# Inverse Haar column transforms of the first 16 channels moved to VectorE, half of the coefficient sums moved to GpSimd

## Chip, cores and metric

The kernel runs on one core of a Trainium2 chip. The metric is device time in microseconds (us) of one execution; lower is better. Four compute engines matter: TensorE (PE; its weight loads are listed as PEld), VectorE (DVE), ScalarE (ACT) and GpSimd (POOL). SyncE's queue (SP) and ACT's queue issue the DMAs.

## What is computed

Input x has shape (4, 64, 256, 256), float32: 4 batches, 64 channels, images of 256 by 256. Four layers follow each other.

- Layers 0, 1 and 3 are the same kind: a long two-dimensional convolution of each channel with a separable filter that a small sine network makes, plus the input times a bias per channel. As the filter is separable, it is two one-dimensional causal convolutions, one along each axis.
- Layer 2 goes through a two-dimensional Haar transform:

```python
f1 = haar2d(x)
for i in range(2):
    f4 = einsum('bchw,oc->bohw', f1 * v[i], conv_w[i])
    acc = acc + sign(f4) * relu(abs(f4) - tau[i])
y = haar2d(acc, inverse=True) + x
```

So each coefficient position mixes the 64 channels by two 64 by 64 matrices, each of the two results is soft-thresholded, and the two are added.

## The kernel before

A convolution of layers 0, 1 or 3 along one axis is one `contract` (two pairs of matmuls against a Toeplitz tile read from DRAM), so a layer takes two: `a` then `y`. ACT copies the first product out of PSUM (L275), VectorE adds the residual to the second (L292).

For each batch b there are three stages.

**convolutions(b)**: per channel, layers 0 and 1 (`a0`, `y0`, `a1`, `y1`), then the Haar transform along rows on VectorE (lengths 128 and 64, L350 and L351) and on GpSimd (lengths 32 to 2, the same two lines, ten instructions for each four channels), then along columns on TensorE (`down`, tile `pz`, with the numbers split by ACT and VectorE into two fp32r parts, `sp`). Coefficients go to DRAM (`coef`), sums and differences for later (`keep`).

**mixing(b)**: 64 groups g of two coefficient rows each (q = 0, 1). Per group: TensorE multiplies by the two matrices (`px`), VectorE and ACT scale (L468, L473), ACT takes the absolute value into `mag` (L477) and the sign (L480), VectorE subtracts the threshold (`shrink`, L484) and multiplies by the sign (`signed`, L488). `add` (L494) sums the two terms into `z`, one instruction of 128 by 256 for each q, both on VectorE. The tile `mag` has two buffers, so the Abs of group g + 2 needs the adds of group g. `z` holds a whole batch in SBUF: four chunks of 16 channels, 128 coefficient rows, 256 columns' worth in each partition.

**inverse(b)**: the inverse Haar transform along columns, in two different ways:

- Channels 16 to 63 (chunks 1 to 3 of `z`): VectorE does it in place in `z`. `level(n, chunk)` is one of seven steps, n = 1, 2, 4 ... 64; it works on n pairs of rows with two instructions in `halve` (L299, L300). An instruction covers up to 16 pairs here, 128 by 1024.
- Channels 0 to 15 (chunk 0): no levels. After the row transform, `halves` splits the PSUM result into two fp32r parts (ACT cast L548, VectorE subtraction L549, tile `w`), and `cols` multiplies both by a matrix (TensorE L555, tile `pu`, two matmuls of 512 columns per channel). This takes one tick more before the join.

Per channel c: `fetch` copies the channel's column from `z` (ACT, L534), `rows` does the row transform on TensorE (L541, L542, tile `pw`), `join` combines it with `r`, loaded from `keep` (VectorE L563, L566, L567), and layer 3 follows (`a3`, `y3`), with the result stored. In batches 0 to 2 every third channel from 2 on stops after the join; its result is stored to `late`, and layer 3 for these 63 images runs alongside the mixing of batch 3 (tile `v`).

**Order.** Every step is put into a list with a time in ticks (`at`; the offsets are the table `PLACE`), sorted and emitted. The order in the list is a priority: a scheduler then lays out each engine's instructions, and an instruction whose inputs are there may be placed ahead of others that wait. While batch b is mixed, the convolutions of batch b + 1 run beside it; a group of the mixing takes one tick, a channel of the inverse too. `along` is the tick at which the mixing of the batch starts, `start` the tick at which its inverse starts.

Of the kernel before, what the change touches and what calls it, by code (L numbers as in the profile page):

```python
# [12 lines left out]
ALU = mybir.AluOpType  # L13
# [3 lines left out]
B, C, S, EMB, ORD = 4, 64, 256, 33, 64  # L17
# [8 lines left out]
PLACE = {  # L26
    "load": 0.714,
    "a0": 1.643,
    "a0 copy": 1.643,
    "y0": 2.571,  # L30
    "y0 sum": 2.571,
    "a1": 3.5,
    "a1 copy": 3.5,
    "y1": 4.429,
# [63 lines left out]
def conv_seq_kernel(ctx, tc, x, fz, fw, bias, decay, haar, haar_row, factors, vt, taut, wmix, out):  # L98
# [14 lines left out]
    nc = tc.nc  # L113
# [22 lines left out]
    z = zpool.tile([P, 4, P, 4, 16], F32, name="z")  # L136
# [21 lines left out]
    order = mybir.DependencyInfo(mybir.DependencyClass.NoSync, mybir.DependencyReason.DATA)  # L158
# [135 lines left out]

        return [product, residual]

    def halve(even, odd):

        nc.vector.tensor_sub(odd, even, odd)  # L299
        nc.vector.scalar_tensor_tensor(even, even, 2.0, odd, ALU.mult, ALU.subtract)  # L300

    def level(n, chunk, begin=0, count=None):

        count = n if count is None else count
        v = z.rearrange("p n s x c -> p n s (x c)")[:, chunk].rearrange("p (j e s) x -> p j e s x", e=2, s=P // 2 // n)
        halve(v[:, begin : begin + count, 0, 0, :], v[:, begin : begin + count, 1, 0, :])

    def butterfly():

        v = z.rearrange("p n s (h k) c -> p n s h k c", k=2)  # L310
        for h in range(2):
            halve(v[:, :, 0, h, 0, :], v[:, :, 0, h, 1, :])
# [6 lines left out]
    def at(time, run, unit):  # L319
        events.append((time, len(events), run, unit))  # L320
# [104 lines left out]
    def mixing(b, start, n_act):  # L425

        st = {}

        def load(g):
            f = mx.tile([P, 2, S], F32, name=f"f_{b}_{g}", tag="f", bufs=3)  # L430
            nc.sync.dma_start(f, coef[b].rearrange("k c p w -> (k c) p w")[:, 2 * g : 2 * g + 2])
            st[g] = {"f": f}
            if g % GT == 0:
                t = mx.tile([P, 2, GT, 16], F32, name=f"vt_{b}_{g}", tag="vt")
                nc.sync.dma_start(t, scales[g // GT])
                st["vt", g // GT] = t

        def scale(g, i):
            return st["vt", g // GT][:, i, g % GT, :]

        def over(g, i, n):
            return scale(g, i)[:, :n].unsqueeze(2).to_broadcast([P, n, C])

        def mix(g):
            f = st[g]["f"]
            ps = psx.tile([P, 2, 2, S], F32, name=f"px_{b}_{g}", tag="mix")
            for q in range(2):
                for h in range(2):
                    nc.tensor.matmul(  # L449
                        ps[:, q, h, :],  # L450
                        f[:, q, h * P : (h + 1) * P],
                        wb.rearrange("p r n -> p (r n)"),
                        start=True,
                        stop=True,
                    )
            if g == 0:

                one, two = ps[:, 0, :, :P], ps[:, 0, :, P:]
                d = mx.tile([P, 2, P], F32, name=f"d_{b}", tag="mag")
                nc.vector.tensor_copy(d, two)  # L460
                nc.vector.tensor_sub(two, one, d)
                nc.vector.tensor_add(one, one, d)
            st[g]["f4"] = mx.tile([P, 16, C], F32, name=f"f4_{b}_{g}", tag="f4")
            st[g]["px"] = ps.rearrange("p q h (r i o) -> p (q h r i) o", r=2, i=2)

        def scaled(g):
            px, n = st[g]["px"], 16 - n_act
            nc.vector.tensor_tensor(st[g]["f4"][:, :n], px[:, :n], over(g, 0, n), ALU.mult)  # L468

        def scaled_too(g, half):  # L470
            px, f4 = st[g]["px"], st[g]["f4"]
            for j in range(16 - n_act + half * (n_act // 2), 16 - (1 - half) * (n_act - n_act // 2)):
                nc.scalar.mul(f4[:, j], px[:, j], scale(g, 0)[:, j : j + 1])  # L473

        def size(g):
            mag = st[g]["mag"] = mx.tile([P, 16, C], F32, name=f"mag_{b}_{g}", tag="mag")
            nc.scalar.activation(mag, st[g]["f4"], AF.Abs)  # L477

        def sign(g):
            nc.scalar.activation(st[g]["f4"], st[g]["f4"], AF.Sign)  # L480

        def shrink(g):
            mag = st[g]["mag"]
            nc.vector.tensor_sub(mag, mag, over(g, 1, 16))  # L484

        def signed(g):
            mag = st[g]["mag"]
            nc.vector.scalar_tensor_tensor(mag, mag, 0.0, st[g]["f4"], ALU.max, ALU.mult)  # L488

        def add(g):  # L490
            parts = st.pop(g)["mag"].rearrange("p (q x i) (n c) -> p q i x n c", q=2, i=2, n=4)
            for q in range(2):
                to = slot(2 * g + q)
                nc.vector.tensor_add(  # L494
                    z[:, :, to].rearrange("p n x c -> p x n c"), parts[:, q, 0], parts[:, q, 1]
                )


        for g in range(S // 4):
            for name, stage in zip(  # L500
                ("mix load", "mix", "scaled", "scaled too", "scaled rest", "size", "sign", "shrink", "signed", "add"),
                (
                    load,
                    mix,
                    scaled,
                    lambda g: scaled_too(g, 0),
                    lambda g: scaled_too(g, 1),
                    size,
                    sign,
                    shrink,  # L510
                    signed,
                    add,
                ),
            ):
                at(start + g + PLACE[name if b + 1 < B else "l " + name], stage, g)

    def inverse(b, start, put_off):

        st = {}

        def early(c):
            tag, bufs = ("f", 3) if c < 20 or c % 5 < 3 else ("f4", 2)
            r = mx.tile([P, 2, 2, P], F32, name=f"r_{b}_{c}", tag=tag, bufs=bufs)
            nc.sync.dma_start(r, keep[b][c])
            st[c]["r"] = r
# [34 lines left out]
        def join(c):  # L560
            ps = st[c]["pw"]
            t = io.tile([P, 2, 2, P], F32, name=f"t_{b}_{c}", tag="res", bufs=BUFS["res"])
            nc.vector.scalar_tensor_tensor(t, st[c]["r"], 0.5, ps, ALU.mult, ALU.add)  # L563
            u = io.tile([P, 2, S], F32, name=f"u_{b}_{c}", tag="y", bufs=BUFS["y"])
            v = u.rearrange("p m (w e) -> p m w e", e=2)
            nc.vector.tensor_add(v[:, :, :, 0], t[:, 0], t[:, 1])  # L566
            nc.vector.tensor_sub(v[:, :, :, 1], t[:, 0], t[:, 1])  # L567
            st[c]["u"] = u
# [4 lines left out]
        along = start - groups - 3  # L573

        def when(tick, n, chunk, *span):
            at(tick + PLACE["level"], lambda _: level(n, chunk, *span), 0)

        at(along + 11 + PLACE["level"], lambda _: butterfly(), 0)
        for chunk in range(1, 4):
            turn = start + 16 * (chunk - 1)  # L580
            for n in (1, 2, 4, 8):
                when(along + 12 + 3 * chunk if b + 1 < B else turn, n, chunk)
            when(turn + 1, 16, chunk)
            for i in range(2):
                when(turn + 2 + 2 * i, 32, chunk, 16 * i, 16)
            for i in range(4):
                when(turn + 6 + 2 * i, 64, chunk, 16 * i, 16)

        for c in range(C):
            for name, stage in zip(("sooner", "early", "fetch", "rows"), (sooner, early, fetch, rows)):  # L590
                at(start + c + PLACE[name], stage, c)
            turn = start + c
            if c < 16:
                at(start + c + PLACE["halves"], halves, c)
                at(start + c + PLACE["cols"], cols, c)
                turn += 1
            at(turn + PLACE["join"], join, c)
            if c in put_off:
                at(turn + PLACE["aside"], aside, c)
            else:  # L600
                shift = (0.0, 0.0)
                if put_off:
                    shift = ((-0.27, -0.342), (0.23, 0.158))[c % 3]
                for name, stage in zip(("a3", "a3 copy", "y3", "y3 sum", "out"), last(b, st)):
                    at(turn + PLACE[name] + shift[name[0] != "a"], stage, c)
# [59 lines left out]
    ahead = C  # L665
    start = ready + 3
    for b in range(B):
# [10 lines left out]
        start = max(end + C, ready + 3)  # L678
        ahead = start - 3
# [114 lines left out]
```

## Time and profile before

| | us |
|---|---|
| median of 3 runs | 2875.76 |
| lowest, highest | 2874.41, 2878.55 |
| the profiled execution, time | 2874.07 |
| the profiled execution, span of the trace | 2872.3 |
| PE busy | 2827.1 |
| DVE busy | 2494.9 |
| ACT busy | 2080.3 |
| POOL busy | 334.4 |

The page lists for each engine how long it was busy; the span is what the trace covers, the time includes what lies around it (1.8 us). Groups of instructions are listed by line, engine and tile, with the number of instructions, the busy time, the mean duration in ns, and the idle time before them with what ended it. A line of a timeline has the start, the time until the end of the last of the merged instructions, the engine, the line, what is written from what is read, and how many instructions it merges. A window's row has the busy time of each engine in that window.

### The profile page before, as it was taken

To read this page: it belongs to the slowest core of one execution; us is meant where nothing else is said; L and a number is where in the kernel's file an instruction comes from. 1 tells how busy PE (TensorE), PEld (TensorE's weight loads), DVE (VectorE), ACT (ScalarE), POOL (GpSimd) and SP (SyncE) were. 2 spreads that over 40 slices of the span, in tenths; PEclk is the share of its full clock that TensorE was granted. 3 is DMA by queue.
4 is the path that set the end of the run, shared out by engine and by line. 5 is a ranking of instruction groups with operands and counts; after the bars stand their busy time and mean duration, and the time that the engine had idled before them with its cause. 6 is when DMAs were issued, how large, how long until landed. Compare 5 with 4: busy or idle time off the path is not lost. (4 is left out here: it accounts for less than half of the span.)

```text
span 2872.3 us, 52434 instructions
## 1 busy us (share of the span) xinstructions
PE 2827.1 (98%) x16592; PEld 2555.6 (89%) x16592; DVE 2494.9 (87%) x4255; ACT 2080.3 (72%) x4950; POOL 334.4 (12%) x644
## 2 busy tenths in 40 slices
PE   9999999999999999999999999999999999999999
PEld 7899998898888898998898998998898998888998
DVE  4655558999999779999999779999999779999985
ACT  2333338999995558998985658999995659998554
POOL 0111111121121001221221001121121000000000
PEclk9999999999999999999999999999999999999999
DMA  6878787776667986777777986777777988787786
GB/s 182 249 231 230 232 232 227 207 208 204 205 209 213 289 254 198 214 213 214 209 207 236 299 255 196 213 214 216 208 208 235 297 266 235 229 238 212 224 241 201
DMA packets 599367, 649.77 MB, mean 226 GB/s; under 512 B 48465, under 2 KB 517044, under 8 KB 598964
## 3 DMA queue, kind: packets, MB, share of 16 engines
q1 hardware_dynamic: 536996, 578.61, 68.9%
q10 hardware_dynamic: 62096, 67.82, 6.7%
q8 instruction: 134, 2.20, 0.3%
q14 instruction: 141, 1.16, 0.1%
HBM read 426.77 MB, written 219.48 MB: 225 GB/s over the span
## 5 line engine op out<-in xcount | busy, mean ns | idle before, releaser
L261 PE MATMUL py<-t,a 128*128 128x256 f32 x3072 | 922.5, 382 | 9.5 <-ACT a L275 8.7
L275 ACT COPY a<-pa 128x512 f32<-128x512 f32 x768 | 478.8, 623 | 498.6 <-PE pa L262 455.2
L473 ACT ACTIVATE f<-px,vt 128x64 f32<-128x64 f32 x2816 | 610.5, 367 | 101.6 <-DVE f L468 101.1
L262 PEld LDWEIGHTS py<-t,a 128*128 128x128 f32 x3072 | 583.4, 190 | 79.3
L262 PE MATMUL py<-t,a 128*128 128x128 f32 x3072 | 590.0, 274 | 0.0
L261 PEld LDWEIGHTS py<-t,a 128*128 128x128 f32 x3072 | 497.3, 191 | 51.2 <-ACT a L275 19.0
L449 PE MATMUL px<-wb,f 128*128 128x256 f32 x2048 | 487.6, 380 | 7.6 <-ACT f L473 7.6
L449 PEld LDWEIGHTS px<-wb,f 128*128 128x128 f32 x2048 | 369.0, 190 | 50.0 <-ACT f L473 10.5
L351 POOL TENSOR_TENSOR sd<-less 128x128 f32<-128x128 f32 (+4 forms) x320 | 190.8, 596 | 1858.7 <-DVE less L350 1519.9
L534 ACT COPY zc<-z 128x512 f32<-128x512 f32 x256 | 282.1, 1105 | 108.1 <-PE pw L542 99.0
L484 DVE TENSOR_TENSOR mag<-mag,vt 128x1024 f32<-128x1024 f32 x256 | 316.6, 1237 | 12.3 <-ACT mag L477 11.5
L488 DVE SCALAR_TENSOR_TENSOR mag<-mag,f 128x1024 f32<-128x1024 f32 x256 | 316.6, 1238 | 0.0
L261 PE MATMUL pa<-t,y 128*128 128x256 f32 x1024 | 309.1, 384 | 6.8 <-DVE y L292 5.2
L261 PE MATMUL pa<-t,x 128*128 128x256 f32 x1024 | 305.9, 381 | 0.5 <-DMA t<-pad 0.5
L477 ACT ACTIVATE mag<-f 128x1024 f32<-128x1024 f32 x256 | 295.7, 1155 | 2.8 <-DVE z L494 0.4
L374 DVE TENSOR_TENSOR sp<-sd,sp 128x512 fp32r<-128x512 f32 x256 | 179.8, 702 | 129.3 <-ACT sp L369 128.2
L480 ACT ACTIVATE f<-f 128x1024 f32<-128x1024 f32 x256 | 285.8, 1116 | 3.5
L261 PE MATMUL pa<-t,u 128*128 128x256 f32 x772 | 233.2, 384 | 6.5 <-ACT w L548 2.8
L292 DVE SCALAR_TENSOR_TENSOR y<-x,bsb,py 128x512 f32<-128x512 f32 x256 | 190.9, 746 | 41.9 <-PE py L262 41.0
L262 PEld LDWEIGHTS pa<-t,x 128*128 128x128 f32 x1024 | 194.6, 190 | 26.3
L262 PEld LDWEIGHTS pa<-t,y 128*128 128x128 f32 x1024 | 194.5, 190 | 26.3
L292 DVE SCALAR_TENSOR_TENSOR y<-y,bsb,py 128x512 f32<-128x512 f32 x256 | 190.7, 745 | 26.0 <-PE py L262 25.6
(73 smaller groups left out, 4412.3 us busy)
## 6 DMA issues: line engine op xcount, KB each, us to landing
t<-pad SPq DMA_DIRECT2D x768, 256.0 KB, 4.1
x<-in_x SPq DMA_DIRECT2D x256, 256.0 KB, 3.7
coef<-co SPq DMA_DIRECT2D x256, 256.0 KB, 3.2
f<-coef SPq DMA_DIRECT2D x256, 256.0 KB, 3.2
r<-keep SPq DMA_DIRECT2D x256, 256.0 KB, 4.1
out_y<-y ACTq DMA_DIRECT2D x193, 256.0 KB, 4.3
keep<-sums SPq DMA_DIRECT2D x256, 128.0 KB, 2.8
keep<-sd SPq DMA_DIRECT2D x256, 128.0 KB, 2.8
```

The source lines that it names most:

```text
L261: nc.tensor.matmul(ps[:, m, :], src[:, 0, m * P : (m + 1) * P], t[:, ::-1], start=True, stop=False)
L262: nc.tensor.matmul(ps[:, m, P:], src[:, 1, m * P : (m + 1) * P], t[:, : P - 1 : -1], start=False, stop=True)
L275: nc.scalar.copy(a, s["p" + new])
L292: nc.vector.scalar_tensor_tensor(y, s[res], bsb[:, layer, c : c + 1], s["p" + new], ALU.mult, ALU.add)
L351: engine.tensor_tensor(t[:, :, :, half:length], v[..., 0], v[..., 1], ALU.subtract)
L449: nc.tensor.matmul(ps[:, q, h, :], f[:, q, h * P : (h + 1) * P], wb.rearrange("p r n -> p (r n)"), start=True, stop=True,)
L473: nc.scalar.mul(f4[:, j], px[:, j], scale(g, 0)[:, j : j + 1])
L477: nc.scalar.activation(mag, st[g]["f4"], AF.Abs)
L480: nc.scalar.activation(st[g]["f4"], st[g]["f4"], AF.Sign)
L484: nc.vector.tensor_sub(mag, mag, over(g, 1, 16))
L488: nc.vector.scalar_tensor_tensor(mag, mag, 0.0, st[g]["f4"], ALU.max, ALU.mult)
L534: nc.scalar.copy(a.rearrange("p h k i -> p (h k) i"), z[:, c // 16, :, :, c % 16].rearrange("p i x -> p x i"))
```

## The change

In batches 0 to 2, chunk 0 gets levels like the other three, and `halves` and `cols` are no longer emitted for channels 0 to 15; their join is one tick earlier. The last batch keeps `halves` and `cols`. The levels of batches 0 to 2 get new places: all levels of chunk 0 but the last eight pairs, those of chunk 1 up to half of n = 64, and those of chunks 2 and 3 up to n = 16 are placed within the mixing; the rest within the inverse, in pieces of 8 pairs (128 by 512). From `start` on, a piece gets a scheduling order (no semaphore) behind the last join emitted before it. In the mixing of batches 0 to 2, the add of q = 1 goes to GpSimd for all groups but the last two; in batch 3 both adds do. The buffers for `r` use tag `f4` from channel 4 on instead of channel 20 in batches 0 to 2.

```diff
-    def halve(even, odd):
+    behind = [None]
+    order = mybir.DependencyInfo(mybir.DependencyClass.NoSync, mybir.DependencyReason.DATA)
 
-        nc.vector.tensor_sub(odd, even, odd)
+    def halve(even, odd, stay=False):
+
+        first = nc.vector.tensor_sub(odd, even, odd)
+        if stay and behind[0] is not None:
+            tc.add_manual_dep(first.ins, behind[0].ins.name, order, reason="not ahead of the joins")
         nc.vector.scalar_tensor_tensor(even, even, 2.0, odd, ALU.mult, ALU.subtract)
...
                 to = slot(2 * g + q)
-                nc.vector.tensor_add(
-                    z[:, :, to].rearrange("p n x c -> p x n c"), parts[:, q, 0], parts[:, q, 1]
-                )
+                engine = nc.gpsimd if g + 2 < S // 4 and (q or b + 1 == B) else nc.vector
+                engine.tensor_add(z[:, :, to].rearrange("p n x c -> p x n c"), parts[:, q, 0], parts[:, q, 1])
...
-            tag, bufs = ("f", 3) if c < 20 or c % 5 < 3 else ("f4", 2)
+            tag, bufs = ("f", 3) if c < (4 if b + 1 < B else 20) or c % 5 < 3 else ("f4", 2)
...
-            nc.vector.scalar_tensor_tensor(t, st[c]["r"], 0.5, ps, ALU.mult, ALU.add)
+            behind[0] = nc.vector.scalar_tensor_tensor(t, st[c]["r"], 0.5, ps, ALU.mult, ALU.add)
...
+        def piece(tick, n, chunk, begin, count):
+            at(tick + PLACE["level"], lambda _: level(n, chunk, begin, count, stay=tick >= start), 0)
+
         at(along + 11 + PLACE["level"], lambda _: butterfly(), 0)
-        for chunk in range(1, 4):
-            turn = start + 16 * (chunk - 1)
-            for n in (1, 2, 4, 8):
-                when(along + 12 + 3 * chunk if b + 1 < B else turn, n, chunk)
-            when(turn + 1, 16, chunk)
-            for i in range(2):
-                when(turn + 2 + 2 * i, 32, chunk, 16 * i, 16)
+        if b + 1 < B:
+            for chunk in range(4):
+                for n in (1, 2, 4, 8):
+                    when(along + 12 + 3 * chunk, n, chunk)
+                when(along + 20 + 3 * chunk, 16, chunk)
+            for chunk in range(2):
+                for i in range(2):
+                    when(along + 37 + i + 3 * chunk, 32, chunk, 16 * i, 16)
+                for i in range(3 - chunk):
+                    when(along + 43 + 8 * i + 3 * chunk, 64, chunk, 16 * i, 16)
+            when(along + 63, 64, 0, 48, 8)
+            when(start - 0.2, 64, 0, 56, 8)
             for i in range(4):
-                when(turn + 6 + 2 * i, 64, chunk, 16 * i, 16)
+                piece(start + 4 + 2 * i, 64, 1, 32 + 8 * i, 8)
+            for chunk in range(2, 4):
+                turn = start + 20 * chunk - 32
+                for i in range(4):
+                    piece(turn + i, 32, chunk, 8 * i, 8)
+                for i in range(8):
+                    piece(turn + 4 + 2 * i, 64, chunk, 8 * i, 8)
+        else:
+            for chunk in range(1, 4):
...
-            if c < 16:
+            if c < 16 and b + 1 == B:
                 at(start + c + PLACE["halves"], halves, c)
                 at(start + c + PLACE["cols"], cols, c)
                 turn += 1
```

The branch behind the last `else` is the old placing of chunks 1 to 3, now for the last batch alone.

More of the change, by code (lines that the diff above doesn't have):

```diff
@@ L295, in second, with level @@
         return [product, residual]
-    def halve(even, odd):
-        nc.vector.tensor_sub(odd, even, odd)
+    behind = [None]
[4 more added lines that the diff above has]
+            tc.add_manual_dep(first.ins, behind[0].ins.name, order, reason="not ahead of the joins")
         nc.vector.scalar_tensor_tensor(even, even, 2.0, odd, ALU.mult, ALU.subtract)
-    def level(n, chunk, begin=0, count=None):
+    def level(n, chunk, begin=0, count=None, stay=False):
         count = n if count is None else count
         v = z.rearrange("p n s x c -> p n s (x c)")[:, chunk].rearrange("p (j e s) x -> p j e s x", e=2, s=P // 2 // n)
-        halve(v[:, begin : begin + count, 0, 0, :], v[:, begin : begin + count, 1, 0, :])
+        halve(v[:, begin : begin + count, 0, 0, :], v[:, begin : begin + count, 1, 0, :], stay)
     def butterfly():
@@ L576, in when @@
             at(tick + PLACE["level"], lambda _: level(n, chunk, *span), 0)
+        def piece(tick, n, chunk, begin, count):
+            at(tick + PLACE["level"], lambda _: level(n, chunk, begin, count, stay=tick >= start), 0)
         at(along + 11 + PLACE["level"], lambda _: butterfly(), 0)
-        for chunk in range(1, 4):
-            turn = start + 16 * (chunk - 1)
-            for n in (1, 2, 4, 8):
-                when(along + 12 + 3 * chunk if b + 1 < B else turn, n, chunk)
-            when(turn + 1, 16, chunk)
-            for i in range(2):
-                when(turn + 2 + 2 * i, 32, chunk, 16 * i, 16)
-            for i in range(4):
-                when(turn + 6 + 2 * i, 64, chunk, 16 * i, 16)
+        if b + 1 < B:
[10 more added lines that the diff above has]
+            when(start - 0.2, 64, 0, 56, 8)
+            for i in range(4):
+                piece(start + 4 + 2 * i, 64, 1, 32 + 8 * i, 8)
[7 more added lines that the diff above has]
+            for chunk in range(1, 4):
+                turn = start + 16 * (chunk - 1)
+                for n in (1, 2, 4, 8):
+                    when(turn, n, chunk)
+                when(turn + 1, 16, chunk)
+                for i in range(2):
+                    when(turn + 2 + 2 * i, 32, chunk, 16 * i, 16)
+                for i in range(4):
+                    when(turn + 6 + 2 * i, 64, chunk, 16 * i, 16)
         for c in range(C):
```

## The prediction, made before the change was run

> **What bounds the kernel now.** I read the page's busy shares first, then the stages, then single instructions.
>
> ```profile
> PE 2827.1 (98%) x16592; PEld 2555.6 (89%) x16592; DVE 2494.9 (87%) x4255; ACT 2080.3 (72%) x4950; POOL 334.4 (12%) x644
> PEclk9999999999999999999999999999999999999999
> ```
>
> TensorE is busy 98% at the full granted clock, so only less TensorE work or less TensorE idling can shorten the run. To see how near the other engines are, I cut the trace at the first Abs (L477) of a mixing, its last add into z (L494), the fetch of channel 16, and the next mixing. Columns: window, length, then busy time of PE, PEld, DVE, ACT, POOL, clock, DMA share, GB/s. The rows are mixing 0, inverse 0 up to channel 16, its rest, mixing 1, inverse 1 up to channel 16, mixing 3.
>
> ```profile
> 452.30:856.20 403.90, 398.21 (x2203) 355.13 (x2202) 397.99 (x667) 379.50 (x1085) 79.39 (x120) 1.00 0.70 207
> 856.20:924.60 68.40, 62.69 (x389) 55.89 (x388) 67.96 (x111) 39.25 (x59) 10.01 (x20) 1.00 0.69 210
> 924.60:1067.70 143.10, 140.67 (x917) 129.50 (x916) 107.59 (x205) 81.70 (x112) 0.00 (x0) 0.99 0.89 273
> 1067.70:1510.30 442.60, 440.38 (x2474) 396.67 (x2473) 434.50 (x722) 394.10 (x1106) 88.03 (x140) 1.00 0.72 209
> 1510.30:1576.70 66.40, 64.28 (x403) 58.35 (x402) 59.87 (x107) 39.39 (x60) 7.60 (x20) 1.00 0.76 232
> 2361.70:2639.00 277.30, 268.15 (x1452) 239.31 (x1451) 275.64 (x403) 264.93 (x691) 0.00 (x0) 1.00 0.79 231
> ```
>
> In mixing 0 and 1 VectorE is as full as TensorE. Much of that is filling: the same windows for L299 and L300 alone show 18.45 + 17.24 = 35.7 us of level work in mixing 0 and 25.61 + 24.70 = 50.3 in mixing 1, although only some 8 us of either has a place there in the code: levels are pulled forward into free VectorE time. TensorE idles mainly in inverse 0 before channel 16 (68.40 - 62.69 = 5.7 us, VectorE full) and in mixing 3 (9.15 us, VectorE full).
>
> **Part 1: TensorE loses `cols`.** The timeline of PE around one channel:
>
> ```profile
> 1527.00 0.71 PE L555 MATMUL pu<-w,hb 128*128 128x512 f32 x2
> 1527.55 0.59 PE L261 MATMUL py<-t,a 128*128 128x256 f32 x2
> ```
>
> Durations overlap (0.71 us), but the next matmul starts 0.55 us after the pair, and that is what the pair occupies. 16 channels in 3 batches go: 48 x 0.55 = 26.4 us from a saturated engine, so all of it on the path. With them go 48 ACT casts (L548, 590 ns) and 48 VectorE subtractions:
>
> ```profile
> L549 DVE TENSOR_TENSOR w<-pw,w 128x512 fp32r<-128x512 f32 x64 | 43.6, 686 | 0.2 <-ACT w L548 0.2
> L299 DVE TENSOR_TENSOR z<-z 128x1024 f32<-128x1024 f32 (+4 forms) x140 | 122.4, 887 | 0.2
> ```
>
> Back to back, VectorE instructions start 0.09 us before the one before ends, so 686 ns is 0.60 of queue and the 1024-element form (1227 ns alone) 1.14: VectorE loses 16 x 0.60 = 9.6 us per inverse.
>
> **Part 2: VectorE gains chunk 0's levels.** Per batch: n = 16, 32, 64 are 14 full-size instructions, 14 x 1.14 = 16.0 us; n = 1 to 8 add 2 x (0.13 + 0.20 + 0.335 + 0.60) = 2.5; 18.5 in all. The diff's places give mixing: chunk 0 but for its last piece 17.3, chunk 1 up to half of n = 64 13.9, chunks 2 and 3 up to n = 16 9.6: 40.8 us. The rest (pieces of 0.60 us an instruction, held behind the last join) goes to the inverse: 13.2 before channel 16 (1.2 + 4.8 + 4.8 + 2.4), 21.6 after it.
>
> **Part 3: GpSimd gets one add of two** (62 groups in three batches, both adds in the last: 186 + 124 = 310). Two adds take VectorE 0.67 us (2576.20 to 2576.87 below), so 62 x 0.335 = 20.8 us per early mixing, 41.5 in the last. The trace has no add of 256 elements on GpSimd. Its nearest rows are levels of 64 and 128 elements, alone and against VectorE (three places of the timeline):
>
> ```profile
> 711.21 3.86 POOL L351 TENSOR_TENSOR sd<-less 128x128 f32<-128x128 f32 x1 [27.67 <-DVE less L350]
> 711.30 1.24 DVE L484 TENSOR_TENSOR mag<-mag,vt 128x1024 f32<-128x1024 f32 x1
> 712.44 2.38 DVE L488 SCALAR_TENSOR_TENSOR mag<-mag,f 128x1024 f32<-128x1024 f32 x2
> 714.71 0.44 DVE L468 TENSOR_TENSOR f<-px,vt 128x256 f32<-128x256 f32 x1
> ...
> 1309.15 0.40 POOL L351 TENSOR_TENSOR sd<-less 128x128 f32<-128x128 f32 x1 [21.02 <-DVE less L350]
> 1309.22 0.88 DVE L374 TENSOR_TENSOR sp<-sd,sp 128x512 fp32r<-128x512 f32 x1 [0.21 <-ACT sp L369]
> ...
> 1313.02 0.29 POOL L351 TENSOR_TENSOR sd<-less 128x64 f32<-128x64 f32 x1
> ```
>
> 0.29 for 64 and 0.40 for 128 make an estimated 0.62 for 256 when free. When VectorE runs one instruction after another with both inputs in SBUF, GpSimd waits for one that reads PSUM (L468, L292): 3.86 us. VectorE pays little: the L374 beside the 0.40 us op took 0.88 against a mean 0.702, 0.18 more. For twice the elements I bound it by 0 (beside a PSUM reader) and 0.36, and take half, as most but not all VectorE time has two SBUF inputs: 62 x 0.18 = 11 us per mixing, at most 22.
> A rule speaks against this part: the Trainium skill's page "SBUF — State Buffer", section "Who interferes with whom", says that a VectorE instruction with two SBUF inputs and a GpSimd instruction that reads SBUF exclude each other, the later one blocked fully. With the 2.6 cycles per element of its page "GPSIMD Engine Reference" (section 3.1), an estimated 0.55 us per add, VectorE could lose 0.55 for each 0.335 saved, 186 x 0.215 = 40 us worse over the three mixings. The 0.18 us above agrees with the exclusion and puts its price on VectorE far lower.
>
> VectorE's account, from the windows: mixing 0: 398.0 - 35.7 - 20.8 + 40.8 + 11 = 393 of 403.9 (382 at no interference, 404 at 0.36 an add); mixing 1: 434.5 - 50.3 - 20.8 + 40.8 + 11 = 415 of 442.6 (404 to 426); inverse 0 before channel 16 (22 us of levels and 9.6 of halves out, 13.2 in): about 50 in a window shortened to about 60; after it 107.6 - 3.7 - 1.4 + 21.6 = 124 of 143. It fits everywhere, narrowly in mixing 0. Gain in inverse 0: between 0 and its 5.7 us of idling, taken as 3, as the cast and subtraction in the chain go.
>
> **Who waits for the adds.** The level that reads group 39 is placed 1.27 ticks (8 us) behind its add, and the freed `mag` buffer is wanted by the Abs two groups on. For chunk 0's last level (1.2 us) and a late add at the start of an inverse: the last add of mixing 0 ended at 856.2 and the first `pw` matmul came at 864.6, so 7 us of other matmuls cover it; uncovered, three starts of up to 5 us would cost 15. On GpSimd's own queue the adds stand among the ten level instructions of each four channels; the cast `sp` (L369) that needs those waited 8.1 us in the whole run, and may wait as much again. For all delays in early mixings I charge 3 us, between 0 and the 14 of rival 1.
>
> The last mixing (VectorE timeline):
>
> ```profile
> 2576.20 0.85 DVE L494 TENSOR_TENSOR z<-mag 128x256 f32<-128x256 f32 x2
> 2576.87 1.31 DVE L488 SCALAR_TENSOR_TENSOR mag<-mag,f 128x1024 f32<-128x1024 f32 x1
> 2578.00 0.84 DVE L292 SCALAR_TENSOR_TENSOR y<-v,bsb,py 128x512 f32<-128x512 f32 x1
> 2578.66 0.78 DVE L468 TENSOR_TENSOR f<-px,vt 128x512 f32<-128x512 f32 x1
> 2579.26 1.31 DVE L484 TENSOR_TENSOR mag<-mag,vt 128x1024 f32<-128x1024 f32 x1
> ```
>
> These five fill a group's 4.19 us without a gap: VectorE sets the pace. Without the adds it needs 3.52; TensorE was busy 96.7% of this window and ACT 95.5%, 4.05 and 4.0 us of a group, and they become the pace. Gain between 0 and 9 us (TensorE's idling there); I take 5.
>
> **Sum.** 26.4 + 3 + 5 - 3 = 31.4 off the profiled execution's 2874.07 us gives 2842.7; the median of the runs lies 1.7 above that execution: 2844. Ends with the same mechanism: 26.4 + 5.7 + 9 gives 2835, and 26.4 - 11 gives 2860.
>
> **Rivals.**
> 1. *VectorE becomes the bound of the early mixings.* If each add costs VectorE 0.36 and the level pieces wait for late adds, mixing 0 overruns by some 5 and inverse 0 keeps its idling; with stalls of 1 to 2 us at the eight or so n = 64 levels, 14 us in all: 2844 + 3 + 14 = 2861. For: 398 of 404 us now. Against: mixings 1 and 2 have 28 us room.
> 2. *The TensorE gain is hidden: the first 16 joins wait for `r`.* Joins, a3 to y3 and the DMAs behind them (`out`, `aside`, on ACT's queue) come a tick earlier, while the loads on SP's queue keep their place; from channel 4 on they gain the `f4` buffers that `w` held.
>
> ```profile
> DVE t L563 <- DMA r<-keep: 9.9, 10, 1.1
> ```
>
> Ten waits of 1 us each now. 0.55 us at each of the 48 joins would eat the 26.4: about 2872, no change. Against: the channels after 16 already join with that lead, and lose little.
> 3. *Slower: GpSimd's two adds come late in the last mixing.* Now the Abs follows 3.35 us after the end of the L488 two groups before (2573.99 to 2577.34). In the new order GpSimd has the 1.26 us of L292 and L468 free, 2 x 0.62 just fits. If one add misses it and is blocked as in the 3.86 us row, `mag` is free 4.7 us after L488, 1.35 late; both blocked, 7.7. With two buffers that is paid every second group: 31 x 1.35 = 42 us, up to 135. The first: 2844 + 5 + 42 = 2891. It decides from 4.35 us on (31 x 1.0 = the whole gain). For: 1.24 in 1.26. Against: in the trace only runs of two-SBUF instructions block, and y or `scaled` comes every 4.2 us.
>
> **How the numbers follow.** A measurement here tells 0.2% (5.75 us) from no change: 2870 to 2881.5. Forecast (2832 to 2858) 0.66, rival 1 (2858 to 2870) 0.14, rival 2 0.06, rival 3 0.14. Faster 0.80, same 0.06, slower 0.14. The range 2832 to 2872 takes in the forecast, rival 1 and the near edge of rival 2, some 0.81; rival 3 and the rest of rival 2 are left out.
>
> **What would show it.** Right: L555 and L549 fall to 32 and 16; PE busy falls by about 26 and its share stays 98%; mixings 0 to 2 keep their lengths within 5 us, each inverse before channel 16 is 8 us shorter; the last mixing nears 270. Adds on POOL average 0.7 to 2 us. Wrong: ACT L477 waiting for POOL z; VectorE's L300 waiting for POOL z; a last mixing over 277; L563 waiting for `r` more than 20 times.

## The result: 1.5% slower, and the profile after

The changed kernel takes 2920.11 us (median; 2917.66 to 2927.69) against 2876.36 for the kernel before: a ratio of 1.0154 [1.0138, 1.017], 43.8 us slower. The forecast was 2844. The profiled execution took 2927.69 us, 7.6 above its median; the table has 8.0 us more in the stage ahead of the first mixing, where the change does nothing.

The page after: busy shares, and the group of the adds that GpSimd took over.

```profile
PE 2834.4 (97%) x16496; PEld 2541.7 (87%) x16496; DVE 2476.5 (85%) x4053; ACT 2060.2 (70%) x4902; POOL 620.0 (21%) x954
...
L500 POOL TENSOR_TENSOR z<-mag 128x256 f32<-128x256 f32 x310 | 306.8, 1002 | 1187.3 <-DVE mag L493 1182.7
```

The work moved as the diff says: 310 adds are on POOL, with a mean of 1.00 us each. (The lines of the changed kernel stand three to six further down: Abs L482, the subtraction L489 and the product L493 on `mag`, add L500, levels L302 and L305, join L567 to L571.) Of TensorE's 128 `cols` matmuls (46.5 us busy before) the 32 of the last batch are left:

```profile
L559 PE MATMUL pu<-w,hb 128*128 128x512 f32 x32 | 11.3, 434 | 0.0
```

The stages, cut at the same events as before: mixing 0, inverse 0 up to channel 16, mixing 1, inverse 1 up to channel 16, mixing 3 (columns: window, length, busy time of PE, PEld, DVE, ACT, POOL, clock, DMA share, GB/s).

```profile
460.30:873.10 412.80, 400.69 (x2201) 355.26 (x2200) 400.80 (x619) 380.40 (x1084) 139.89 (x182) 1.00 0.68 202
873.10:936.10 63.00, 57.63 (x359) 51.15 (x357) 52.51 (x101) 32.63 (x44) 3.41 (x11) 1.00 0.79 242
...
1079.60:1530.00 450.40, 440.85 (x2458) 394.64 (x2457) 423.17 (x660) 394.30 (x1104) 140.72 (x202) 1.00 0.69 205
1530.00:1597.00 67.00, 62.69 (x388) 55.66 (x386) 54.95 (x106) 33.23 (x46) 3.26 (x11) 1.00 0.82 242
...
2398.00:2694.80 296.80, 273.30 (x1448) 237.72 (x1447) 285.96 (x318) 266.89 (x691) 123.78 (x124) 1.00 0.74 216
```

All four mixings are longer, and only inverse 0 is shorter by more than 3 us. In mixing 1 VectorE is 11 us less busy than before and yet the mixing is 7.7 us longer; TensorE's gap there (length less busy time) went from 2.2 to 9.6 us. In mixing 3 it went from 9.2 to 23.5. The same cut of every kernel's trace, in us, with both parts of an inverse together; "levels part" is the change without GpSimd, "adds part" the kernel before with GpSimd's adds alone (both told below):

| stage | before | after | levels part | adds part |
|---|---|---|---|---|
| ahead of mixing 0 | 452.3 | 460.3 | 454.4 | 457.5 |
| mixing 0 | 403.8 | 412.9 | 418.6 | 414.1 |
| inverse 0 | 211.5 | 206.5 | 204.1 | 202.8 |
| mixing 1 | 442.7 | 450.4 | 439.7 | 451.8 |
| inverse 1 | 206.1 | 211.0 | 210.1 | 207.5 |
| mixing 2 | 442.6 | 450.4 | 439.8 | 451.8 |
| inverse 2 | 202.6 | 206.6 | 205.8 | 203.5 |
| mixing 3 | 277.3 | 296.9 | 277.4 | 297.5 |
| inverse 3 | 233.3 | 231.1 | 232.7 | 230.6 |

From mixing 0 on, after less before makes 45.7 us: mixings +9.1, +7.7, +7.8, +19.6; inverses -5.0, +4.9, +4.0, -2.3.

The waits of the changed kernel, waiter and releaser, then total us, count, longest us:

```profile
PE pa L261 <- DVE y L292: 26.6, 39, 1.7
PE py L261 <- ACT a L275: 24.2, 30, 1.8
DVE z L302 <- POOL z L500: 15.7, 15, 2.2
ACT mag L482 <- POOL z L500: 15.1, 10, 2.1
```

TensorE's first two were 5.2 and 8.7 us before:

```profile
PE pa L261 <- DVE y L292: 5.2, 11, 1.4
```

The last two of the changed kernel are new. They are two of the signs named for "wrong": a level and the Abs wait for a GpSimd add. The Abs does so in mixings 0 to 2 alone (4.1, 5.5 and 5.5 us); in the last mixing no Abs waits for an add, and levels wait 5.2 us. A wait of the join (L567) for `r` is not among the waits, so rival 2 is out.

### The profile page after: what moved, and what is told of

It is laid out like the page before. It is cut to its first block, busy times and chain, and to the rows that moved or that the text cites. A ratio compares the mean times of both kernels' runs of the same rounds, so it can differ in the third digit from the quotient of the medians.

```text
span 2925.9 us, 52426 instructions
## 1 busy us (share of the span) xinstructions
PE 2834.4 (97%) x16496; PEld 2541.7 (87%) x16496; DVE 2476.5 (85%) x4053; ACT 2060.2 (70%) x4902; POOL 620.0 (21%) x954
## 5 line engine op out<-in xcount | busy, mean ns | idle before, releaser
L275 ACT COPY a<-pa 128x512 f32<-128x512 f32 x768 | 471.8, 614 | 531.1 <-PE pa L262 475.4
L261 PEld LDWEIGHTS py<-t,a 128*128 128x128 f32 x3072 | 494.3, 191 | 75.4 <-ACT a L275 45.7
L500 POOL TENSOR_TENSOR z<-mag 128x256 f32<-128x256 f32 x310 | 306.8, 1002 | 1187.3 <-DVE mag L493 1182.7
L356 POOL TENSOR_TENSOR sd<-less 128x128 f32<-128x128 f32 (+4 forms) x320 | 177.6, 555 | 816.7 <-DVE less L355 698.3
L261 PE MATMUL pa<-t,y 128*128 128x256 f32 x1024 | 313.5, 388 | 31.1 <-DVE y L292 26.6
L489 DVE TENSOR_TENSOR mag<-mag,vt 128x1024 f32<-128x1024 f32 x256 | 321.2, 1255 | 25.8 <-ACT mag L482 25.3
L493 DVE SCALAR_TENSOR_TENSOR mag<-mag,f 128x1024 f32<-128x1024 f32 x256 | 318.9, 1246 | 0.9
L482 ACT ACTIVATE mag<-f 128x1024 f32<-128x1024 f32 x256 | 291.0, 1137 | 20.6 <-POOL z L500 15.1
```

The lines of the kernel that those rows point to most:

```text
L261: nc.tensor.matmul(ps[:, m, :], src[:, 0, m * P : (m + 1) * P], t[:, ::-1], start=True, stop=False)
L275: nc.scalar.copy(a, s["p" + new])
L500: engine.tensor_add(z[:, :, to].rearrange("p n x c -> p x n c"), parts[:, q, 0], parts[:, q, 1])
```

## Experiments

Two theories stood at the start: GpSimd's adds cost the time (G), or the levels that VectorE gained do (L).

### 1. The change without GpSimd's adds

```diff
-                engine = nc.gpsimd if g + 2 < S // 4 and (q or b + 1 == B) else nc.vector
+                engine = nc.vector
```

> The change with all adds back on VectorE: the new level places and the missing column matmuls stay. Theory G (the GpSimd adds cost the time: 8 us in each early mixing, 20 in the last): mixings 0 to 2 back at about 404, 443 and 443 us, the last at 277, total 2920 - 44 = 2876, give or take 5. Rival L (chunk 0's levels in the mixings and the order of the inverses cost it): early mixings stay at 413 and 450, total 2920 - 20 = 2900.

Measured: 2884.36 us, 1.0024 [1.0013, 1.0034], 7.2 us slower than before. So 36 of the 44 us go with the adds, but the other part, forecast as nearly the whole gain, isn't a gain at all. Mixing 0 and inverse 1 up to channel 16 of this kernel:

```profile
454.40:873.00 418.60, 403.86 (x2206) 357.37 (x2205) 408.54 (x681) 381.04 (x1086) 77.91 (x120) 0.99 0.68 201
...
1516.80:1583.20 66.40, 62.12 (x385) 55.11 (x383) 54.89 (x105) 33.08 (x45) 3.28 (x11) 1.00 0.81 244
```

Neither forecast total is met. Theory L holds for mixing 0 alone: VectorE is busy 408.5 of 418.6 us, and the mixing is 15 longer. Mixings 1 and 2 are 3 us shorter, mixing 3 unchanged. Inverse 1 up to channel 16 keeps its 66.4 us although 16 `cols` have gone from TensorE.

### 2. GpSimd's adds alone, in the kernel before; and without the last mixing's

The first of the two is the kernel before with the change's add and its `engine` line; the second is the change with

```diff
-                engine = nc.gpsimd if g + 2 < S // 4 and (q or b + 1 == B) else nc.vector
+                engine = nc.gpsimd if g + 2 < S // 4 and q and b + 1 < B else nc.vector
```

> The kernel before with the GpSimd adds of the change alone: no chunk 0 levels, the column matmuls and casts stay. Theory G: the early mixings grow by about 8 us each and the last by 20, total 2876 + 44 = 2920. Rival L: only the last mixing grows, 2896. The prediction's own account (GpSimd adds relieve VectorE) would give 2865 to 2870.

> The change with the last mixing's adds back on VectorE; GpSimd keeps one add of two in the first three. Theory G: only the last mixing changes, from 297 to 277 us, total 2900. Rival L gives the same here; were the time lost by something that the last mixing inherits from the stage before, it would stay near 297 and the total near 2920.

Measured: 2918.97 us for the adds alone, 1.0146 [1.0131, 1.0161], 41.8 us slower; 2902.21 for the change without the last mixing's adds, 1.009 [1.0075, 1.0105], which is 17.9 less than the changed kernel. The two parts by themselves give 7.2 + 41.8 = 49.0, the change 43.8: they add up to within 5.2 us. Theory G named both totals within 3 us. In the adds part mixings 1 to 3 are as long as after the change, within 1.4 us.

### 3. What GpSimd's adds cost while VectorE is relieved of nothing

The kernel before, and after VectorE's own add the same number of adds on GpSimd (310):

```diff
+                if g + 2 < S // 4 and (q or b + 1 == B):
+                    same = z[:, :, to].rearrange("p n x c -> p x n c")
+                    nc.gpsimd.tensor_add(same, same, same)
```

> The kernel before with 310 GpSimd adds more, at the groups of the change: VectorE's adds stay and release mag as before, then GpSimd adds the same row of z to itself, so that the affected terms are doubled in the output. VectorE's order of work is that of the kernel before. Theory K (GpSimd's reads lock VectorE out, a few tenths of a us each time): the early mixings grow by 8 to 15 us each and the last by 20 to 35, total 2920 to 2955. Rival M (the locks are small, late release of mag is what costs): every mixing within 4 us of before, total below 2890.

Measured: 2929.64 us, 1.0183 [1.0168, 1.0198]. VectorE runs the same instructions in each mixing, in mixing 0 in the order of the kernel before, in mixing 3 too but for a handful; in mixings 1 and 2 the order differs in part. Mixings 0 to 2 grew by 8.5, 9.8, 9.8 us, mixing 3 by 28.8, as theory K had it: divided by 62 and 124 adds, 0.14 to 0.16 us for an add in the early mixings and 0.23 in the last. In mixing 3 VectorE is busy 304.4 us instead of 275.6, 28.7 of the 28.8. The timeline of that last mixing (start, duration, engine):

```profile
2501.20 0.74 DVE L494 TENSOR_TENSOR z<-mag 128x256 f32<-128x256 f32 x2
...
2501.69 2.28 POOL L499 TENSOR_TENSOR z<-z 128x256 f32<-128x256 f32 x2 [2.33 <-DVE z L494]
...
2501.87 1.63 DVE L488 SCALAR_TENSOR_TENSOR mag<-mag,f 128x1024 f32<-128x1024 f32 x1
```

The L488 that runs beside GpSimd's pair takes 1.63 us where the same operation alone takes 1.22: 0.4 us beside a pair of adds. GpSimd's pair takes 2.28 us; the shortest single add of this kernel took 0.61. VectorE is held inside the instruction (called a lock below); the waits show little of it (levels wait 7.1 us for adds in the whole run, 0.5 in mixing 3).

### 4. The same relief, without the adds' duration

The adds part of experiment 2, each GpSimd add cut to 16 of its 256 elements (`z` is zero-filled once, early):

```diff
-                engine.tensor_add(z[:, :, to].rearrange("p n x c -> p x n c"), parts[:, q, 0], parts[:, q, 1])
+                few = slice(0, 1) if engine is nc.gpsimd else slice(0, 4)
+                engine.tensor_add(
+                    z[:, few, to, :1 if engine is nc.gpsimd else 4].rearrange("p n x c -> p x n c"),
...
+        for i in range(64):
+            at(24 + i / 2, lambda _, i=i: nc.gpsimd.memset(room[:, 512 * i : 512 * i + 512], 0.0), 0)
```

> The kernel before with the GpSimd adds of the change alone (2919 us), each add on GpSimd cut to 16 of its 256 elements (the rest of those sums is missing; z is filled with zeros once, early in the first stage). Levels are pulled forward as in that variant. Theory K (the length of GpSimd's reads costs, by locks and by late ends): early mixings at 443 us or less, last mixing 277 or less, total 2862 to 2880. Rival F (levels pulled forward into the freed time and the other order of instructions cost): last mixing above 285, total above 2895.

Measured: 2879.06 us, 1.0018 [1.0001, 1.0034]. Its profiled execution took 2893.19, 14 above the median; its first stage, with the fills, is 18.5 us longer than that of the kernel before, and all later stages together 0.6 longer. Mixings 1 and 3:

```profile
1077.40:1518.90 441.50, 437.98 (x2454) 393.85 (x2453) 418.68 (x658) 393.88 (x1104) 116.59 (x202) 1.00 0.70 208
2372.70:2659.00 286.30, 268.13 (x1442) 237.46 (x1441) 276.51 (x316) 265.30 (x691) 37.63 (x124) 1.00 0.77 223
```

Two readings. With the adds short, mixings 0 to 2 are back at 403.3, 441.5 and 441.3 us: their lengthening came from how long each add holds, and the relief of VectorE, which is still there in full, is worth 0.5 to 1.3 us of a mixing and, through levels done earlier, 8.3 us of inverse 0 (inverses 1 and 2 are 1.4 and 2.4 longer). And the last mixing stays 9 us longer even so; what the small adds still hold is in that too. The total and the early mixings are as theory K had them, the last mixing is as rival F had it.

### 5. The last mixing: levels held back, and one add of two

VectorE's new free time in the last mixing was filled: level instructions come in pairs (L302, L305), and the last mixing had 12 pairs before, most of them small (10 us of VectorE's queue), and has 32 after (51 us). The change with the last batch's levels ordered behind its last add:

```diff
-                    when(turn, n, chunk)
+                    piece(turn, n, chunk, 0, n)
...
+                if b + 1 == B and g + 1 == S // 4:
+                    behind[0] = done
```

> The change with batch 3's levels held by a scheduling order behind the last add of the last mixing, so that none is pulled forward into it (33 were in the change, 2 remain). Theory F (the VectorE time that the adds free is filled again by levels pulled forward, so VectorE stays full and GpSimd's locks come on top): the last mixing falls from 297 to 265 to 275 us, total 2890 to 2900, less what the last inverse then pays for 36 levels (up to 15 us). Rival M (the two GpSimd adds free mag too late, rival 3 of the prediction): the last mixing stays above 290, total 2915 to 2925.

Measured: 2913.71 us, 1.0127 [1.0112, 1.0142]: between the two theories. Mixing 3 falls from 296.9 to 285.3, and 3.5 us come back in the last inverse, which now does the levels. So about 11.6 of the 19.6 us are the levels pulled forward, and 8.0 are left with GpSimd's adds, although VectorE is busy 249.1 us there instead of 275.6. Two lines of that mixing (a subtraction as it starts beside a pair of adds):

```profile
2505.48 1.42 POOL L500 TENSOR_TENSOR z<-mag 128x256 f32<-128x256 f32 x2 [3.27 <-DVE mag L493]
2506.26 1.72 DVE L489 TENSOR_TENSOR mag<-mag,vt 128x1024 f32<-128x1024 f32 x1
```

Late ends are not what is left: all 124 adds take 0.72 to 0.74 us, and no Abs waits for one. Locks are there. The pair of adds runs for 0.64 us more when the subtraction L489 starts, and L489 takes 1.72 us instead of 1.21. Of the 64 subtractions 25 overlap no add and take 1.21 to 1.23 us; for the 39 others the time above 1.21 us is the overlap less 0.13 us, 13 us in all. VectorE has 36 us free in this mixing, though, so that these locks make the 8.0 us is not shown. Then the same hold in the kernel before, where VectorE keeps its adds, and that with one add of two on GpSimd:

```diff
+                engine = nc.gpsimd if b + 1 == B and g + 2 < S // 4 and q else nc.vector
```

> The kernel before with batch 3's levels held behind the last mixing, all adds on VectorE. VectorE set the pace of the last mixing (276 of 277 us); 10 us of levels leave it: last mixing 266 to 269, the last inverse 1 to 3 us longer, total 2867 to 2871. Rival: TensorE and ACT are the pace as well, last mixing 274 or more, total 2875 or more.

> The kernel before with batch 3's levels held behind the last mixing and one of its two adds (q = 1) on GpSimd; nothing else of the change. VectorE loses 10 us of levels and 21 us of adds there. If locks alone count (62 x 0.23 us = 14 us on VectorE): last mixing 260 to 268 us, total 2862 to 2869. If the late release of mag counts with one add too: last mixing 275 or more, total 2876 to 2884.

Measured: 2875.92 us for the hold alone, 1.0002 [0.9992, 1.0011]; 2883.79 with one add on GpSimd, 1.0027 [1.0018, 1.0037] (its profiled execution took 2879.16). The last mixing of the first and of the second:

```profile
2362.40:2639.00 276.60, 268.48 (x1443) 237.20 (x1442) 269.70 (x383) 265.23 (x691) 0.00 (x0) 1.00 0.81 231
```

```profile
2361.10:2642.80 281.70, 269.36 (x1442) 235.04 (x1440) 257.99 (x321) 264.46 (x690) 52.91 (x62) 1.00 0.78 226
```

The hold takes 9.5 us of levels out of VectorE's queue, GpSimd's adds take out some 21 more; VectorE is busy 275.6 us before, 269.7 with the hold, and 258.0 with both. The first step leaves the mixing as long as it was (276.6 against 277.3), as the rival had it, and with the second it is 5 longer. VectorE was full there, but it did not set the pace alone. In the hold alone TensorE's `py` matmuls wait 5.5 us for ACT's copies `a` (their weight loads 9.8); TensorE is busy 268.5 and ACT 265.2. The 5 us with one add fall in the range of the second theory, but its mechanism is not in the trace: no Abs waits for a GpSimd add there, and no subtraction or product is stretched (1.23 us at most). What the trace shows is `py` matmuls waiting longer for ACT's copies `a` (11.7 us, weight loads 20.9); why the copies come later stays open.

### 6. The levels part: where 26.4 us of TensorE went

First the kernel before with the casts, subtractions and `cols` of channels 0 to 15 left out in batches 0 to 2, and nothing in their place; then the change without GpSimd (experiment 1) with the level pieces in those batches' inverses left out:

```diff
-            if c < 16:
+            if c < 16 and b + 1 == B:
```

```diff
-            for i in range(4):
-                piece(start + 4 + 2 * i, 64, 1, 32 + 8 * i, 8)
-            for chunk in range(2, 4):
...
-                for i in range(8):
-                    piece(turn + 4 + 2 * i, 64, chunk, 8 * i, 8)
```

> The kernel before with casts, subtractions and column matmuls of channels 0 to 15 left out in batches 0 to 2 and nothing in their place: their column transform is missing. It prices the first part of the prediction alone. If TensorE's 26.4 us are on the path: 2848 to 2853. If the inverse is paced by the joins' chain once the casts are gone (rival Q): 2862 to 2875.

> The variant without GpSimd adds (2884 us), with the level pieces of the three inverses left out as well: the last levels of chunks 1 to 3 in batches 0 to 2 are missing. VectorE has 34 us less in each inverse. Theory P (TensorE's saved 26 us turn into waits because joins stand behind level pieces on VectorE): TensorE's idling in inverse 1 falls from 15 us to about 4, each inverse is 8 to 10 us shorter, total 2855 to 2862. Rival Q (without the cast the join itself holds the PSUM pair that the next channel's row matmuls need, pieces or not): inverses stay within 3 us, total above 2875.

Measured: 2862.23 us without `cols`, 0.9946 [0.9929, 0.9962], which is 14.8 us less than before and not 26.4; 2853.74 without the pieces, 0.9918 [0.9904, 0.9933], 30.6 us less than experiment 1. The first stands at the lower edge of rival Q's range; the second is below theory P's, each inverse 7.5 to 10.8 us shorter, and rival Q's "within 3 us" is out there. Inverse 1 up to channel 16 without `cols`, then without the pieces:

```profile
1514.10:1577.00 62.90, 60.05 (x382) 54.41 (x382) 53.99 (x96) 33.04 (x46) 9.34 (x20) 1.00 0.83 254
```

```profile
1501.70:1564.70 63.00, 61.69 (x395) 56.24 (x394) 47.29 (x91) 33.41 (x46) 6.36 (x20) 1.00 0.88 263
```

Without `cols` inverses 0, 1, 2 are 3.0, 5.3 and 6.7 us shorter, where the forecast had 8.8 for each; inverse 0 up to channel 16 isn't shorter at all (69.9 against 68.4; VectorE is busy 65.5 of it, and the clock granted in this window was 0.95, which can hide some 3 of its 60.8 us of TensorE). What the pieces do is seen in the timeline of experiment 1, in inverse 1:

```profile
1632.76 0.68 DVE L302 TENSOR_TENSOR z<-z 128x512 f32<-128x512 f32 x1
1633.36 0.74 DVE L292 SCALAR_TENSOR_TENSOR y<-u,bsb,py 128x512 f32<-128x512 f32 x1
1634.01 0.68 DVE L305 SCALAR_TENSOR_TENSOR z<-z 128x512 f32<-128x512 f32 x1
1634.62 0.68 DVE L567 SCALAR_TENSOR_TENSOR t<-r,pw 128x512 f32<-128x512 f32 x1
...
1635.44 0.46 PE L545 MATMUL pw<-hrow,zc 128*128 128x128 f32 x2 [0.96 <-DVE t L567]
```

Without the cast, the PSUM pair `pw` is free for the next row matmuls only when the join has read it. The first four lines show a level piece's two instructions (0.60 us of queue each) ahead of a join (L567) in the same queue, the last one TensorE waiting 0.96 us for that join. From channel 16 on, a join of inverse 1 starts 0.98 us after its row matmuls end (mean), without the pieces 0.25 us. TensorE's matmuls wait 5.4 us for joins and their sums in this inverse, without the pieces 1.3. VectorE has 21 us free after channel 16 and still delays TensorE. What hides the rest of the 26.4 us when nothing is put in place of `cols` is traced in part only: in inverse 0 row matmuls then wait 4.8 us in two waits for joins, a wait that the kernel before does not have.

### 7. The levels part mended

Experiment 1 without the ordering behind the joins (`stay=False`), and that with batch 0 left as in the kernel before (the tag of `r` and the old places of its levels too):

```diff
-            at(tick + PLACE["level"], lambda _: level(n, chunk, begin, count, stay=tick >= start), 0)
+            at(tick + PLACE["level"], lambda _: level(n, chunk, begin, count, stay=False), 0)
```

```diff
-        if b + 1 < B:
+        if 0 < b < B - 1:
...
-            if c < 16 and b + 1 == B:
+            if c < 16 and b in (0, B - 1):
```

> The variant without GpSimd adds (2884 us), with the scheduling order behind the joins taken off: 6 more of the level pieces are pulled forward into each of mixings 1 and 2. Theory P: inverses 1 and 2 a few us shorter, mixings 1 and 2 not longer since VectorE has 17 us room there: 2876 to 2882. Rival: pieces ahead of joins delay them more, 2886 to 2895.

> The variant without GpSimd adds and without the order behind the joins (2877 us), with batch 0 as in the kernel before: chunk 0's levels only in batches 1 and 2, where VectorE has room. Theory: in the 2877 us variant mixing 0 was 12 us longer and inverse 0 9 us shorter than before, mixing and inverse 1 together 1 us shorter; so 3 us go here: 2872 to 2875, at the edge of what can be told from the kernel before. If batch 0's longer mixing there was not the levels' doing: 2877 or more.

Measured: 2876.84 us, 1.0001 [0.9992, 1.0011], and 2873.19 us, 0.999 [0.9981, 0.9999]. Letting the scheduler pull pieces into mixings 1 and 2 (38 pairs there instead of 32) takes back the 7 us, as theory P had it; leaving batch 0 alone brings mixing 0 back to 404.2 from 416.0, but gives up 7.6 us in inverse 0. The second is the best version of the computation that was run, 0.1% below the kernel before, less than the 0.2% that the prediction named as what can be told apart.

## Why the prediction was wrong

**Part 1, TensorE loses `cols`: mis-sized.** The work did go: from the first Abs of mixing 1 to that of mixing 2 there are 32 matmuls fewer, two for each of 16 channels. "All of it on the path" was wrong. No matmul runs for 16.8 us there instead of 4.5 (with what the adds do). With nothing put in its place the removal is worth 14.8, not 26.4. Busy 98% said that TensorE was full in the state before; it didn't say how near the next thing was, and the waits that are new in experiment 6 point to the chain join, PSUM pair, row matmul.

**Part 2, "It fits everywhere": the step that failed for the levels.** The account compared sums per window, and the sums were nearly right: after channel 16 in inverse 0, 122.0 us measured against 124; mixing 0, 400.8 against 393. What it left out is the place in the queue. A piece that fits by sum stands ahead of a join that TensorE waits for; 30.6 us is what the pieces cost (experiment 6), charged at nothing. "Narrowly in mixing 0" also failed: levels alone made it 15 us longer, 9.1 with GpSimd's relief. Inverse 0 was to be 8.8 + 3 us shorter and is 5.0 shorter; TensorE's idling in it before channel 16, from which the 3 were to come, stayed (5.7 to 5.4 us).

**Part 3, GpSimd's adds: price about right, set against the wrong account.** The lock was taken as 0.18 us an add; a mixing grew by 0.14 to 0.16 (early) and 0.23 (last) for each. The exclusion of the Trainium skill's page "SBUF — State Buffer", section "Who interferes with whom", is seen in experiments 3 and 5; in the latter VectorE waits for nearly the whole overlap. Per add its price stays far below the estimated 0.55 us worked out from the page's rule, as an add does not always meet such an instruction (25 of the 64 subtractions there met none). What failed is that the locks were set against VectorE's free time and all delays in the early mixings charged at 3 us: those mixings grew by 24.6. The relief did not shorten them either: the adds that left VectorE bought 0.5 to 1.3 us of a mixing (experiment 4) and the time in inverse 0, as TensorE is the bound of those mixings, while the locks delay instructions that TensorE waits for. That last link is argued from the waits for `y` (26.6 us, before 5.2; in mixing 1 8.8, before 1.5, with the short adds 3.3); that the length vanishes with the adds' duration is shown. The Trainium skill's page "Perfetto Trace Analysis", section "Optimizing Scalar/DVE Operations", warns that offloading from VectorE to GpSimd might not help because the two share a port; the 41.8 us of experiment 2 agree.

**The last mixing: "VectorE sets the pace" was wrong.** Five instructions without a gap were read as the bound, but with 9.5 us of levels less on VectorE the length stayed (experiment 5). The forecast -5 became +19.6: about 11.6 from levels that the scheduler pulled into the freed time, 8.0 that stay with GpSimd's adds. VectorE lost 41 us of adds and got 41 us of levels there; it is busy 286.0 us instead of 275.6, as the subtraction L489 takes longer (9 us in all, start to start), and its gaps grow from 1.7 to 10.8 us. Level and lock are seen in the changed kernel's timeline of that mixing (POOL's row is three adds together):

```profile
2519.29 4.17 POOL L500 TENSOR_TENSOR z<-mag 128x256 f32<-128x256 f32 x3
...
2521.66 1.22 DVE L302 TENSOR_TENSOR z<-z 128x1024 f32<-128x1024 f32 x1
2522.79 1.76 DVE L489 TENSOR_TENSOR mag<-mag,vt 128x1024 f32<-128x1024 f32 x1
2524.47 1.21 DVE L305 SCALAR_TENSOR_TENSOR z<-z 128x1024 f32<-128x1024 f32 x1
```

A level pair stands around the subtraction on `mag` in the mixing's queue, and the subtraction takes 1.76 us instead of 1.2 while GpSimd's adds run. The two estimates of the 9 to 12 us (experiments 4 and 5) differ. What makes the 8.0 us stays open: late release of `mag` is not it, locks are there but VectorE has time for them, and one add of two cost 5 us without any lock in the trace.

**The rivals.** Rival 3 had the right sign, and its stage did grow, but not by its mechanism: the Abs waits for POOL `z` 15.1 us in 10 waits, all in mixings 0 to 2, and never in the last mixing, where it priced 31 x 1.35; the early mixings, which it left out, cost 24.6. Rival 1's stalls exist (10.5 us in 9 waits of levels for adds in mixings 0 to 2, against its "eight or so" of 1 to 2 us), but VectorE did not become the bound of mixings 1 and 2 (27 us free in each). Rival 2 didn't occur.

**The signs.** L549's subtractions and L555's matmuls fell as named. GpSimd's adds average 1.00 us, as named. PE busy didn't fall (2827.1 to 2834.4). An explanation from the rows, not tested: a matmul's duration overlaps the next one's (0.71 us against 0.55 of queue for a pair of `cols`), and one with a wait behind it counts in full. That sign was a poor one; the count of matmuls is the better. Of the signs of "wrong", three came (Abs and levels waiting for POOL `z`, a last mixing over 277), the waits for `r` did not.

## What to carry to other kernels

Before an engine is relieved, hold back or leave out some of its work in a trial without putting it elsewhere: if the stage keeps its length, the engine isn't its only bound, however full its timeline is, and freed time in its queue can be filled with work pulled forward. Account for a moved instruction by its place, not by the sum of its engine: ask which consumer stands behind it in the queue, and which buffer that consumer frees. Two engines that exclude each other charge inside their instructions, where hardly a wait shows it; measure it by adding the work, and by shrinking it.

## What the runs showed of the hardware that was not expected

- A GpSimd add of 256 fp32 elements per partition takes 0.72 to 0.74 us when free (all 124 with the levels held, experiment 5), not the 0.62 that was carried on from 64 and 128 elements; two of them, 1.47 us, don't fit into the 1.26 us in which VectorE reads PSUM. One of 16 elements takes 0.21 to 0.22 us.
- Blocked, the same add took up to 2.59 us in the changed kernel.
- Where a GpSimd add already runs, VectorE pays: L488 grew from 1.22 to 1.63 us beside a pair of adds, and with the levels held the subtraction L489 was longer by its overlap with the adds less some 0.13 us, up to 0.54 us. Per added add a mixing grew by 0.14 to 0.16 us (mixings 0 to 2) and by 0.23 (mixing 3).
